# Quantile networks for two tiles at once, with the pieces ordered by a plan

## The chip, the cores and the metric

The kernel runs on one core of one Trainium2 chip. Times are device microseconds (us). The metric is the time of one execution, as the median of several runs; lower is better.

## The reference

The program has two layers on a graph of 4096 nodes with 128 features. Layer 0 is graph attention with 8 heads. Layer 1, where the change lies, takes for each node quantiles over a list of its neighbours, for each feature by itself:

```python
def _L1_gnn_ref(x, A, W, b):
    T, K = 5, 2
    QUANTILES, SELF_RATIO = (0.25, 0.5, 0.75), 0.5
    mask = A != 0
    rank = jnp.cumsum(mask.astype(jnp.int32), axis=1) - 1
    num_nbr = mask.sum(axis=1)
    skip = jnp.where(num_nbr > T, jnp.ceil(num_nbr / K).astype(jnp.int32), jnp.int32(1))
    remove = mask & ((rank + 1) % skip[:, None] == 0)
    keep = mask & ~remove
    n_keep = keep.sum(axis=1)
    vals = jnp.where(keep[:, :, None], x[None, :, :], big)
    svals = jnp.sort(vals, axis=1)
    for q in QUANTILES:
        idx = jnp.maximum(jnp.ceil(q * n_keep).astype(jnp.int32) - 1, 0)
        agg = agg + (1 / 3) * take_along_axis(svals, idx)
    agg = where(n_keep > 0, agg, 0)
    agg = (1.0 - SELF_RATIO) * agg + SELF_RATIO * x
    return agg @ W.T + b + x
```

The adjacency matrix holds a neighbour with probability 1/128, so a node has some 32 neighbours, and a kept list has some 22 to 62 entries.

## The kernel before

Two thirds of the program (searching the adjacency matrix for neighbours, building lists, attention, layer norm) are not touched by the change. They end with the rows of layer 0 written to `x1_d` in memory, and with index lists `idx`, where the nodes have been ordered by their number of neighbours and cut into 32 tiles of 128 nodes. Tile `t` has lists of `2 * HT[t]` places, from 22 (tile 0) over 24 to 42 (tile 30) to 62 (tile 31); shorter lists are padded.

The last stage takes one tile after another. POOL issues one indirect gather for each place of the list (`gather`, L186): each brings one row of 128 floats to each of the 128 partitions, one *slot* of the tile's buffer `vals`. `xs` is the nodes' own row. Five buffers of 42 slots, and one of 62 called `most`, are in rotation; a tile is gathered when an earlier one is done.

A selection network (`selection_network`) then brings the few places that can be a quantile (the *targets*, 3 to 5 for most tiles, 12 and 14 for the shortest and the longest lists) into order. It has 15 or 21 stages. A stage compares slot `i` with slot `i + d` for a set of `i`; where both results are needed later the minimum goes to `i` and the maximum to `i + d` (a two-ended piece, two instructions), else only one is computed. `groups` joins neighbouring slots to regular patterns and `pieces_of` cuts these into pieces of at most `TURN` = 12 slots. For each piece, ACT first copies the low slots to a buffer `low` in PSUM (L1162; left out for one-ended pieces of under 4 slots), and DVE compares `low` with the high slots in place (L1166). `low` comes from a pool of two buffers.

At a tile's end (L1175 to L1188) ACT multiplies each target slot by a weight (0 or a share of 1/6 for each node), and `xs` by 0.5; PE adds these products up by matmuls with the identity (`st_ps`), ACT copies the sum out (`sT`), PE multiplies by the layer's weights and adds `xs` and the bias (`fo_ps`), ACT copies the result (`o`), and POOL scatters it to the output (L195).

All engines run this stage in the order in which the program is written (`manual_schedule`). The order comes from generators: `quantile_out` yields after each stage of the network, and the loop takes turns between up to two running tiles. The second one begins when the first has at most 8 turns left. So where two tiles run, one stage of one is followed by one stage of the other, on ACT as on DVE, and between a tile's last stage and its products there is a stage of the other tile.

Of the kernel before, what the change touches and what calls it, by code (L numbers as in the profile page):

```python
# [9 lines left out]
F32 = mybir.dt.float32  # L10
# [3 lines left out]
ALU = mybir.AluOpType  # L14
AX = mybir.AxisListType
PSUM = bass.MemoryType.PSUM
# [8 lines left out]
P = 128  # L25
N = 4096
D = 128
H = 8
NT = N // P
# [31 lines left out]
    31, 32, 32, 33, 33, 34, 34, 35, 35, 36, 36, 37, 38, 39, 40, 42,  # L61
]
HT = [(c - 1) // 2 for c in CAP]
LMAX = 2 * max(HT)
LMOST = 2 * sorted(HT)[-2]
TURN = 12


R_NUM, R_OWN, R_F1 = L, L + 1, L + 2
# [18 lines left out]
def selection_network(n, targets):  # L88


    t = (n - 1).bit_length()
    stages = []
    p = 1 << (t - 1)
    while p:
        q, r, d = 1 << (t - 1), 0, p
        while True:
            stages.append((d, [i for i in range(n - d) if i & p == r]))
            if q == p:
                break
            d, q, r = q - p, q >> 1, p  # L100
        p >>= 1
    live = set(targets)
    plan = []
    for d, lows in reversed(stages):
        mins = [i for i in lows if i in live]
        maxs = [i for i in lows if i + d in live]
        used = set(mins) | set(maxs)
        touched = used | {i + d for i in used}
        plan.append((d, mins, maxs, sorted(live - touched)))
        live |= touched  # L110
    return plan[::-1]


def groups(slots):

    runs = []
    for s in slots:
        if runs and s == runs[-1][0] + runs[-1][1]:
            runs[-1][1] += 1
        else:  # L120
            runs.append([s, 1])
    out = []
    i = 0
    while i < len(runs):
        b, n = runs[i]
        j = i + 1
        stride = n
        if j < len(runs) and runs[j][1] == n:
            stride = runs[j][0] - b
            while j < len(runs) and runs[j] == [b + stride * (j - i), n]:  # L130
                j += 1
        out.append((b, j - i, stride, n))
        i = j
    return out


def pieces_of(g):


    b, k, stride, n = g  # L140
    if k == 1:
        parts = -(-n // TURN)
        out = []
        for i in range(parts):
            m = (n - sum(p[3] for p in out)) // (parts - i)
            out.append((b, 1, m, m))
            b += m
        return out
    if n >= TURN:
        return [p for i in range(k) for p in pieces_of((b + i * stride, 1, n, n))]  # L150
    parts = -(-k // (TURN // n))
    out = []
    for i in range(parts):
        kk = (k - sum(p[1] for p in out)) // (parts - i)
        out.append((b, kk, stride, n))
        b += kk * stride
    return out


def slots_of(tile_, g):  # L160

    b, k, stride, n = g
    if k == 1:
        return tile_[:, b : b + n, :].rearrange("p s d -> p (s d)")
    v = tile_[:, b : b + (k - 1) * stride + n, :]
    flat = v.rearrange("p s d -> p (s d)")

    return bass.AP(
        tensor=flat.tensor,
        offset=flat.offset,  # L170
        ap=[list(flat.ap[0]), [stride * D, k], [1, n * D]],
    )


def quantile_slots(t):


    ht = HT[t]
    slots = {ht - 1}
    for h in range((LOW[t] + 1) // 2 - 1, ht + 1):  # L180
        slots |= {ht - h + (h + 1) // 2 - 1, ht - h + (3 * h + 1) // 2 - 1}
    return slots


def gather(nc, dst, rows, idx):
    nc.gpsimd.indirect_dma_start(  # L186
        out=dst,
        out_offset=None,
        in_=rows,
        in_offset=bass.IndirectOffsetOnAxis(ap=idx, axis=0),  # L190
    )


def scatter(nc, rows, src, idx):
    return nc.gpsimd.indirect_dma_start(  # L195
        out=rows,
        out_offset=bass.IndirectOffsetOnAxis(ap=idx, axis=0),
        in_=src,
        in_offset=None,
    )  # L200
# [9 lines left out]
def kernel(  # L210
# [15 lines left out]
    nc = tc.nc  # L226
# [10 lines left out]
    ident = const.tile([P, P], F32, name="ident")  # L237
# [197 lines left out]
    kp.release()  # L435


    order = sorted(range(NT), key=lambda t: HT[t])
    order = order[0::2] + order[1::2][::-1]
    with tc.tile_pool(name="late", bufs=1) as late, tc.tile_pool(name="sort", bufs=5) as sp, tc.tile_pool(  # L440
        name="fin", bufs=3
    ) as fp, tc.tile_pool(name="low_ps", bufs=2, space=PSUM) as lp, tc.tile_pool(
        name="fin_ps", bufs=1, space=PSUM
    ) as pp, tc.manual_schedule(engines=ALL):
        wt = late.tile([P, NT, LMAX], F32, name="wt")
        slot_weights(tc, late, jp1, picks, wt)
        waiting = list(order)
        lists, running, outs = [], [], []

        def fetch_list():  # L450
            t = waiting.pop(0)
            n = 2 * HT[t]
            if n > LMOST:
                vals = sp.tile([P, LMAX, D], F32, name="most", bufs=1)
            else:
                vals = sp.tile([P, LMOST, D], F32, name="vals")
            for j in range(n):
                gather(nc, vals[:, j, :], x1_d, idx[:, t, j : j + 1])
            xs = fp.tile([P, D], F32, name="xs", bufs=6)
            gather(nc, xs, x1_d, own_i[:, t : t + 1])  # L460
            lists.append((t, vals, xs))

        def begin():
            t = lists[0][0]
            stages = len(selection_network(2 * HT[t], quantile_slots(t)))
            work = quantile_out(
                tc, lp, fp, pp, *lists.pop(0), wt, ident, ones, WlT, vecs[:, 3, :], outs
            )
            running.append([work, stages])

        for _ in range(5):
            fetch_list()
        while running or lists:
            if lists and (not running or (len(running) == 1 and running[0][1] <= 8)):
                begin()
            for one in list(running):
                one[1] -= 1
                if next(one[0], True):
                    running.remove(one)
                    while outs:  # L480
                        t, o = outs.pop(0)
                        scatter(nc, out, o, own_i[:, t : t + 1])
                    if waiting:
                        fetch_list()


    flag = nc.values_load(total[0:1, 0:1], min_val=0, max_val=1 << 20)  # L487
    with tc.If(flag > 0):
# [650 lines left out]
        )  # L1139


def quantile_out(tc, lp, fp, pp, t, vals, xs, wt, ident, ones, WlT, bl_b, outs):


    nc = tc.nc
    targets = sorted(quantile_slots(t))
    for d, mins, maxs, _ in selection_network(2 * HT[t], targets):
        lows, highs = set(mins), set(maxs)
        kinds = (
            (sorted(lows & highs), (0, d)),  # L1150
            (sorted(lows - highs), (0,)),
            (sorted(highs - lows), (d,)),
        )
        for slots, ends in kinds:
            for g in (p for whole in groups(slots) for p in pieces_of(whole)):
                b, k, stride, m = g
                low, high = slots_of(vals, g), slots_of(vals, (b + d, k, stride, m))
                if k * m >= 4 or len(ends) == 2:
                    kept = lp.tile([P, TURN * D], F32, name="low")[:, 0 : k * m * D]
                    if k > 1:  # L1160
                        kept = kept.rearrange("p (k d) -> p k d", k=k)
                    nc.scalar.copy(kept, low)  # L1162
                else:
                    kept = low
                for end in ends:
                    nc.vector.tensor_tensor(  # L1166
                        high if end else low, kept, high, ALU.max if end else ALU.min
                    )
        yield

    st_ps = pp.tile([P, P], F32, name="st_ps")
    terms = [(vals[:, j, :], wt[:, t, j : j + 1]) for j in targets] + [(xs, 0.5)]
    for i, (v, w) in enumerate(terms):
        u = fp.tile([P, D], F32, name="u", bufs=4)
        nc.scalar.mul(u, v, w)  # L1175
        nc.tensor.matmul(  # L1176
            st_ps, lhsT=u, rhs=ident, start=(i == 0), stop=(i == len(terms) - 1)
        )
    yield
    sT = fp.tile([P, P], F32, name="sT")  # L1180
    nc.scalar.copy(sT, st_ps)
    o_ps = pp.tile([P, D], F32, name="fo_ps")
    nc.tensor.matmul(o_ps, lhsT=sT, rhs=WlT, start=True, stop=False)
    nc.tensor.matmul(o_ps, lhsT=ident, rhs=xs, start=False, stop=False)
    nc.tensor.matmul(o_ps, lhsT=ones[0:1, :], rhs=bl_b[0:1, :], start=False, stop=True)
    yield
    o = fp.tile([P, D], F32, name="o")
    nc.scalar.copy(o, o_ps)  # L1188
    outs.append((t, o))


def general_attention(tc, x, adj, wa, x1_d, f2T_d, consts):
# [223 lines left out]
```

## Time and profile before

| what | us |
|---|---|
| median of 3 runs (3865.35 to 3875.0) | 3873.15 |
| the profiled execution | 3874.47 |
| its span, first to last instruction | 3872.7 |
| DVE busy in the span | 2613.9 |
| POOL busy | 2320.1 |
| ACT busy | 1204.0 |
| PE busy | 747.5 |

The span is cut into 40 slices of 96.8 us. The last stage's first gather is issued at 2047.2 us from the span's start, and its first compare starts at 2076.3. In the page and in the answers of the trace, a row names line, engine and operation, then what is written and read with the number of elements on each of 128 partitions; then the count, and busy time and mean duration. A wait names what ended it.

### The profile page before, as it was taken

To read this page: it belongs to the slowest core of one execution; us is meant where nothing else is said; L and a number is where in the kernel's file an instruction comes from. 1 tells how busy PE (TensorE), PEld (TensorE's weight loads), DVE (VectorE), ACT (ScalarE), POOL (GpSimd) and SP (SyncE) were. 2 spreads that over 40 slices of the span, in tenths; PEclk is the share of its full clock that TensorE was granted. 3 is DMA by queue.
4 is the path that set the end of the run, shared out by engine and by line. 5 is a ranking of instruction groups with operands and counts; after the bars stand their busy time and mean duration, and the time that the engine had idled before them with its cause. 6 is when DMAs were issued, how large, how long until landed. Compare 5 with 4: busy or idle time off the path is not lost. (4 is left out here: it accounts for less than half of the span.)

```text
span 3872.7 us, 17731 instructions
## 1 busy us (share of the span) xinstructions
PE 747.5 (19%) x2799; PEld 466.1 (12%) x2801; DVE 2613.9 (67%) x4953; ACT 1204.0 (31%) x1902; POOL 2320.1 (60%) x2452
## 2 busy tenths in 40 slices
PE   2023143334303231334330110000000010000001
PEld 1011022112202211111220100000000000000001
DVE  6798366657702111522214899999999999999987
ACT  3132123324102122221222433434444444344343
POOL 0676177777736677777756777777763345455520
PEclk9966566557656665666665555555555555555555
DMA  5542234334212122222211111111110011111100
GB/s 182 145 154 76 86 97 128 108 99 118 50 38 49 47 49 49 63 55 57 56 43 46 52 52 52 52 52 52 52 47 25 24 27 39 29 36 40 42 17 3
DMA packets 114202, 241.10 MB, mean 62 GB/s; under 512 B 50880, under 2 KB 67264, under 8 KB 105888
## 3 DMA queue, kind: packets, MB, share of 16 engines
q0 software_dynamic: 76224, 161.01, 16.5%
q10 hardware_dynamic: 12160, 68.49, 5.1%
q1 hardware_dynamic: 25696, 10.38, 1.3%
q14 instruction: 96, 0.79, 0.1%
q8 instruction: 26, 0.43, 0.0%
HBM read 228.53 MB, written 11.18 MB: 62 GB/s over the span
## 5 line engine op out<-in xcount | busy, mean ns | idle before, releaser
L1166 DVE TENSOR_TENSOR vals<-low,vals 128x1024 f32<-128x1024 f32 (+9 forms) x1359 | 1403.0, 1058 | 178.8 <-ACT low L1162 106.1
L186 POOL DMA_INDIRECT G<-xt_d,idx x1096 | 1099.1, 1003 | 470.0 <-issue 325.6
L186 POOL DMA_INDIRECT vals<-x_d,idx x960 | 911.6, 950 | 294.9 <-issue 283.4
L1162 ACT COPY low<-vals 128x1024 f32<-128x1024 f32 (+10 forms) x701 | 607.0, 876 | 983.5 <-DVE vals L1166 925.9
L888 PE MATMUL y<-G,pf 128*64 128x258 f32 (+1 forms) x1184 | 249.3, 492 | 837.6 <-DVE pf L866 765.1
L1176 PE MATMUL st_ps<-ident,u 128*128 128x128 f32 x344 | 83.3, 427 | 1662.5 <-ACT u L1175 1559.5
L195 POOL DMA_INDIRECT out_dram<-o,own_i x32 | 31.8, 993 | 467.2 <-ACT o L1188 462.0
L852 DVE TENSOR_TENSOR z<-G,f1x 128x256 f32<-128x256 f32 (+3 forms) x44 | 21.9, 498 | 418.7 <-DMA G<-xt_d,idx 411.2
L1176 PEld LDWEIGHTS st_ps<-ident,u 128*128 128x128 f32 x344 | 73.8, 320 | 1671.3 <-ACT u L1175 1567.9
L901 ACT COPY raw<-y 32x258 f32<-32x258 f32 (+1 forms) x472 | 172.2, 365 | 315.2 <-PE y L888 219.1
L854 ACT ACTIVATE z<-z 128x256 f32<-128x256 f32 (+3 forms) x60 | 20.0, 334 | 804.1 <-DVE z L853 804.1
L888 PEld LDWEIGHTS y<-G,pf 128*64 128x64 f32 (+1 forms) x1184 | 134.8, 183 | 940.9 <-DVE pf L866 753.1
L589 DVE MAX8 first<-sgn 128x8 f32<-128x128 bf16 x1024 | 209.5, 276 | 1.9
L561 ACT ACTIVATE sgn<-adj_t 128x2048 bf16<-128x2048 int32 x64 | 122.0, 1906 | 152.6 <-DVE first L589 118.0
L792 DVE TENSOR_SCALAR bad<-R 128x1 f32<-128x1 f32 x32 | 4.6, 145 | 209.9 <-DMA R<-rec_d 209.9
L1166 DVE TENSOR_TENSOR most<-low,most 128x1024 f32<-128x1024 f32 (+7 forms) x116 | 131.9, 1167 | 2.6 <-ACT low L1162 0.7
L195 POOL DMA_INDIRECT rec_d<-rec,ranks x32 | 30.9, 967 | 156.1 <-DVE ranks L732 100.1
L949 PE MATMUL o<-hv,W_sb 128*128 128x256 f32 (+1 forms) x208 | 85.9, 537 | 196.2 <-DVE hv L943 196.2
L1166 DVE TENSOR_TENSOR vals<-vals 128x256 f32<-128x256 f32 (+2 forms) x335 | 119.0, 410 | 0.0
L908 DVE TENSOR_SCALAR rden<-raw 128x8 f32<-128x8 f32 x32 | 6.7, 208 | 163.2 <-ACT raw L901 163.2
L601 DVE MAX8 rec<-first 128x8 f32<-128x256 f32 x256 | 108.7, 425 | 6.6
L921 ACT COPY yT<-turned 128x512 f32<-128x512 f32 x64 | 65.3, 1020 | 153.6 <-PE turned L920 147.7
(180 smaller groups left out, 1841.2 us busy)
## 6 DMA issues: line engine op xcount, KB each, us to landing
adj_t<-in_adj_dram ACTq DMA_DIRECT2D x64, 1024.0 KB
G<-xt_d,idx POOLq DMA_INDIRECT x1096
vals<-x_d,idx POOLq DMA_INDIRECT x960
R<-rec_d SPq DMA_DIRECT2D x128, 26.4 KB
xt_d<-rec SPq DMA_DIRECT2D x4, 548.0 KB
rec<-in_x_dram SPq DMA_DIRECT2D x4, 512.0 KB
score<-rec_d SPq DMA_DIRECT2D x120, 1.0 KB
Gs<-xt_d,idx POOLq DMA_INDIRECT x88
```

Source lines behind the costliest of these rows:

```text
L186: nc.gpsimd.indirect_dma_start(out=dst, out_offset=None, in_=rows, in_offset=bass.IndirectOffsetOnAxis(ap=idx, axis=0),)
L195: return nc.gpsimd.indirect_dma_start(out=rows, out_offset=bass.IndirectOffsetOnAxis(ap=idx, axis=0), in_=src, in_offset=None,)
L561: nc.scalar.activation(sgn, adj_t, AF.Sign, accum_out=cnt[:, i : i + 1])
L589: nc.vector.max(first[:, ts(c0 // CW + c, 8)], key[:, b * (512 // CW) + c, :])
L601: nc.vector.max(top, first)
L888: nc.tensor.matmul(yv[p0 : p0 + m], lhsT=pf[:, c : c + m], rhs=rhs, start=(i == 0), stop=(i == len(parts) - 1), skip_group_check=True,)
L901: nc.scalar.copy(raw[p0 : p0 + m, 4 * half + b - 1 : 4 * half + b + 1, :], y[p0 : p0 + m, :, a : a + D + 1],)
L921: nc.scalar.copy(yT[:, :, ts(place, P)].rearrange("p h (u g) -> p g u h", u=4)[:, ts(half, 16)], t_ps.rearrange("p b (g u h) -> p (b g) u ...
L949: nc.tensor.matmul(o, lhsT=consts["W1_sb"][:, h, :], rhs=hv[:, ts(j, n)], start=(h == 0), stop=(h == H - 1),)
L1162: nc.scalar.copy(kept, low)
L1166: nc.vector.tensor_tensor(high if end else low, kept, high, ALU.max if end else ALU.min)
L1176: nc.tensor.matmul(st_ps, lhsT=u, rhs=ident, start=(i == 0), stop=(i == len(terms) - 1))
```

## The change

The 32 tiles are put into 19 units: tiles 0, 1, 30, 31, 2 and 3 each by itself, the others two by two. Both tiles of a unit get lists of one length (the longer), lie in one buffer behind one another, and use one network, with the targets of both. A piece holds the same slots of both tiles, up to `TURN` = 14 slots in all, in one instruction; a pattern that would need more pieces that way is cut for each tile by itself. The condition for a copy (at least 4 slots, or two-ended) counts the slots of both tiles.

When the program is built, `plan_units` lays down the order of everything with a small model: what a copy, a compare and a gather take, when each slot is ready, and a ring of two copy buffers. Of the pieces of the current stages of at most two running units it takes the one for which DVE would wait least, the older unit first. When a unit is done, its sums are placed at once, the second half (`turn`) six pieces later, the output copy (`emit`) twelve pieces later, and the next unit's gathers are placed. Output scatters stand among later gathers, one for every fourth. Three buffers of 80 slots take the place of the six. The two copy buffers are halves of one PSUM tile `low`, used by turns; sums and results of both tiles of a unit share one PSUM tile `fin`. `EARLY` is empty, so that `first_stage` is never called.

```diff
+UNITS = [(0,), (1,), (30,), (31,)] + [(t, t + 1) for t in range(28, 3, -2)] + [(2,), (3,)]
+for u in UNITS:
+    for t in u:
+        HT[t] = max(HT[v] for v in u)
 LMAX = 2 * max(HT)
-LMOST = 2 * sorted(HT)[-2]
-TURN = 12
+ROOM = max(2 * HT[u[0]] * len(u) for u in UNITS)
+TURN = 14
+EARLY = []
...
+def stages_of(tiles):
+    n = 2 * HT[tiles[0]]
+    targets = sorted(set().union(*(quantile_slots(t) for t in tiles)))
+    stages = []
+    for d, mins, maxs, _ in selection_network(n, targets):
...
+            for g in groups(slots):
+                whole = [(tuple(range(len(tiles))), p) for p in pieces_of(g, TURN // len(tiles))]
+                apart = [((i,), p) for i in range(len(tiles)) for p in pieces_of(g, TURN)]
+                for who, p in whole if len(whole) <= len(apart) else apart:
+                    stage.append((who, p, d, ends))
+        stages.append(stage)
+    return n, targets, stages
+
+COPY, COMPARE, FETCH, LAND = (150, 107), (110, 133), 1250, 2200
...
+    def best():
+        found = None
+        for r, u in enumerate(running):
+            for p, (who, g, d, ends) in enumerate(todo[u][0]):
+                spots = slots_in(who, g)
+                low = max(at[u, i, s] for i, s in spots)
+                ready = max(at[u, i, s + d] for i, s in spots)
+                copied = len(spots) >= 4 or len(ends) == 2
+                if copied:
+                    done = max(clock["act"], low + 100, ring[0]) + COPY[0] + COPY[1] * len(spots)
+                    ready = max(ready, done + 100)
+                else:
+                    done = clock["act"]
+                    ready = max(ready, low)
+                key = (max(ready - clock["dve"], 0), r, p)
+                if found is None or key < found[0]:
+                    found = (key, u, copied, done)
+        return found
...
+        (late, _, p), u, copied, done = best()
+        who, g, d, ends = todo[u][0].pop(p)
+        events.append(("piece", u, who, g, d, ends, copied))
...
+        if not todo[u]:
+            running.remove(u)
+            events.append(("sums", u))
+            tails += [[count + 6, "turn", u], [count + 12, "emit", u]]
+            clock["act"] = max(clock["act"], clock["dve"]) + 300 * len(UNITS[u]) * (len(plans[u][1]) + 1)
+            free[home[u]] = clock["act"] + 1000
+            if loaded < len(UNITS):
+                load()
...
-    order = sorted(range(NT), key=lambda t: HT[t])
-    order = order[0::2] + order[1::2][::-1]
-    with tc.tile_pool(name="late", bufs=1) as late, tc.tile_pool(name="sort", bufs=5) as sp, tc.tile_pool(
-        name="fin", bufs=3
-    ) as fp, tc.tile_pool(name="low_ps", bufs=2, space=PSUM) as lp, tc.tile_pool(
+    with tc.tile_pool(name="late", bufs=1) as late, tc.tile_pool(name="sort", bufs=3) as sp, tc.tile_pool(
+        name="fin", bufs=2
+    ) as fp, tc.tile_pool(name="low_ps", bufs=1, space=PSUM) as lp, tc.tile_pool(
...
+        plans, events = plan_units(3)
+        work, outs, turn = {}, [], 0
+        low = lp.tile([P, 2, TURN * D], F32, name="low")
+        for kind, u, *rest in events:
+            tiles = UNITS[u]
+            n, targets, stages = plans[u]
+            if kind == "load":
+                vals = sp.tile([P, ROOM * D], F32, name="vals")
...
+                        gather(nc, dst, x1_d, idx[:, t, j : j + 1])
...
+                        if outs and count % 4 == 0:
+                            scatter(nc, out, *outs.pop(0))
+                    gather(nc, xs[:, i, :], x1_d, own_i[:, t : t + 1])
...
+            elif kind == "piece":
+                compare(nc, low[:, turn % 2, :], work[u][0], n, *rest)
+                turn += rest[-1]
+            elif kind == "sums":
+                vals, _, xs, _ = work[u]
+                fin = pp.tile([P, 4, P], F32, name="fin")
+                for i, t in enumerate(tiles):
+                    terms = [
+                        (slots_of(vals, n, (i,), (j, 1, 1, 1)), wt[:, t, j : j + 1]) for j in targets
+                    ] + [(xs[:, i, :], 0.5)]
+                    for a, (v, w) in enumerate(terms):
+                        g = fp.tile([P, D], F32, name="u", bufs=12)
+                        nc.scalar.mul(g, v, w)
+                        nc.tensor.matmul(fin[:, i, :], lhsT=g, rhs=ident, ...)
...
+def compare(nc, room, vals, n, who, g, d, ends, copied):
+    b, k, stride, m = g
+    low, high = slots_of(vals, n, who, g), slots_of(vals, n, who, (b + d, k, stride, m))
+    kept = low
+    if copied:
+        kept = room[:, 0 : len(who) * k * m * D]
...
+        nc.scalar.copy(kept, low)
+    for end in ends:
+        nc.vector.tensor_tensor(high if end else low, kept, high, ALU.max if end else ALU.min)
```

## The prediction

> **What bounds the kernel now.** First the page: whole-span shares, then the slices.
>
> ```profile
> PE 747.5 (19%) x2799; PEld 466.1 (12%) x2801; DVE 2613.9 (67%) x4953; ACT 1204.0 (31%) x1902; POOL 2320.1 (60%) x2452
> ...
> DVE  6798366657702111522214899999999999999987
> ```
>
> DVE works 67% of the span, but from slice 23 on (2227 us) its digit is 9: the last stage, the quantile networks, is DVE's. So I read that stage by stretches (columns PE, PEld, DVE, ACT, POOL).
>
> ```profile
> 2076.00:2400.00 324.00, 27.83 (x108) 23.00 (x108) 282.09 (x312) 125.34 (x174) 245.59 (x258) 0.51 0.20 52
> 2400.00:3780.00 1380.00, 100.58 (x380) 83.06 (x380) 1284.65 (x1415) 572.33 (x767) 762.11 (x802) 0.51 0.14 38
> 3780.00:3862.00 82.00, 8.30 (x33) 6.98 (x33) 73.05 (x98) 30.49 (x50) 1.91 (x2) 0.54 0.00 2
> ```
>
> From the first compare (2076) to the last (3861) DVE works 1639.8 of 1786 us; ACT and POOL have a third to spare. DVE sets the end: 11 us after its last compare the span is over. The waits of the stage (sum, times, longest):
>
> ```profile
> ACT low L1162 <- DVE vals L1166: 954.1, 532, 19.8
> ...
> DVE vals L1166 <- ACT low L1162: 106.1, 135, 4.5
> ...
> DVE vals L1166 <- DMA vals<-x_d,idx: 45.8, 2, 36.0
> ```
>
> ACT waiting for DVE is harmless. DVE waiting for ACT's copies, 106.8 us with the long tile's 0.7, is what an order can win; of the 45.8 behind gathers, 36.0 precede the first compare and stay.
>
> **What one piece costs.** The groups by shape:
>
> ```profile
> L186 POOL DMA_INDIRECT vals<-x_d,idx x919 | 872.9, 950 | 280.6 <-issue 271.2 <-DMA vals<-x_d,idx 6.4 <-DVE vals L1166 3.1
> L1166 DVE TENSOR_TENSOR vals<-low,vals 128x1024 f32<-128x1024 f32 x536 | 646.0, 1221 | 53.1 <-ACT low L1162 32.8 <-DMA vals<-x_d,idx 9.8
> L1162 ACT COPY low<-vals 128x1024 f32<-128x1024 f32 x266 | 267.9, 1015 | 339.7 <-DVE vals L1166 324.4 <-DMA vals<-x_d,idx 8.0 <-DVE most L1166 7.0
> ...
> L1166 DVE TENSOR_TENSOR vals<-vals 128x256 f32<-128x256 f32 x188 | 70.4, 418 | 0.0
> ```
>
> A slot is 128 elements: from 2 to 8 slots a compare grows by (1221-419)/6 = 133.7 ns a slot. Walking the network code for all 32 tiles gives 1823 compares of 10,766 slots and 761 copies, just the counts in the trace. Of the 1786 us, 106.8 + 9.8 are waits and 1439 is slots (10,766 x 0.1337); the other 230 us are 126 ns for each instruction. The same walk over the changed lists, in 19 units: 1383 compares of 10,881 slots, 714 copies of 5692 (before 5149).
>
> **1. Fewer, larger compares.** 440 compares fewer x 0.126 = -55; 115 slots more (equal list lengths) x 0.134 = +15: -40. 168 of those removed are one-ended pieces, cheaper than the mean (two `vals<-vals` of 256 lie 0.33 apart, only 0.07 above their slots), so I take **-37** (-54 to -30). [...]
>
> **2. Sums of two tiles right behind a unit's last compare.** ACT is in order. A tile's end now:
>
> ```profile
> 2678.87 0.75 DVE L1166 TENSOR_TENSOR vals<-vals 128x128 f32<-128x128 f32 x2
> 2679.54 1.41 DVE L1166 TENSOR_TENSOR vals<-low,vals 128x512 f32<-128x512 f32 x2
> ...
> 2679.72 1.28 ACT L1175 ACTIVATE u<-vals,wt 128x128 f32<-128x128 f32 x4 [2.53 <-DVE vals L1166]
> ...
> 2681.00 0.31 ACT L1175 ACTIVATE u<-xs 128x128 f32<-128x128 f32 x1
> 2681.22 1.43 ACT L1162 COPY low<-vals 128x1536 f32<-128x1536 f32 x1
> ...
> 2682.68 1.76 DVE L1166 TENSOR_TENSOR vals<-low,vals 128x1536 f32<-128x1536 f32 x1 [1.74 <-ACT low L1162]
> ```
>
> The tile's last compare ends at 2679.62. ACT then multiplies (four plus one, 0.32 us apart), then copies the other tile's next piece; DVE is covered by one pair (1.41) and idles 1.74. I sum all gaps over 0.1 us at the 31 such ends: 40 us, 4.5 of it at the longest list with its 15 products. In the new order (I walked what follows what, and took no time from the planner's clock) the sums stand directly after the last compare: no copy for the other unit is ahead of them, so the cover is gone, and a double unit has 8 to 12 products. With 2 early, 8 x 0.32 + 0.1, then a copy of 4 to 12 slots (0.59 to 1.44): 3.7 x 13 = 48. The single units: 13 and 15 products 5.8 and 6.0, the others 2.9, 3.2 and 2.3: 20. Together 68, **+27** (10 to 40).
>
> **3. The order.** DVE's other gaps sum to 84: 29 up to 2400, 55 later. At the start units 0, 1 and 30 run nearly alone (30's first piece needs its last gather, at 2161, when 0 and 1 are done): some 7 each as for the first tile now, 26 with 31 and a gather. Later two units hide each other's copies; 2 us per unit for its last small stages is 26, and 5 for the tail. One loss: pairs of 2-slot one-ended pieces, which needed no copy, become 4-slot ones that do; ACT at 0.66 a copy against DVE's 0.60 costs some 0.07 each, 89 times, 6. So 63 instead of 84: **-21** (0 to -50).
>
> **4. Two copy buffers in one PSUM tile.** `low` is [2, 14*128] floats: a half is 7168 bytes, 3.5 banks of 2 KB, so the halves share the fourth bank. Now each buffer is 12 slots, three whole banks. The second half always touches the shared bank, the first half with 14 slots only; by the walked order that is 20 of the 40 14-slot pieces. Are accesses kept apart by byte or by bank? A nearby row:
>
> ```profile
> 1456.50 1.12 PE L981 MATMUL turned<-ident,hv 128*128 128x128 f32 x4
> ...
> 1457.66 0.29 DVE L987 TENSOR_TENSOR x<-turned,R 128x128 f32<-128x128 f32 x1 [1.99 <-PE turned L981]
> ```
>
> Four transposes write four quarters of one bank; DVE reads the first quarter, done after about a quarter of 1.12 us, only once all four are over (1457.62). [...] the trace has only PE against DVE. By byte this costs 0. By bank each of the 20 is bared twice: its own copy (1.65, the 12-slot row plus two slots) waits for the compare before it, and the next copy (0.59 to 1.65) for its own compare: with 0.1 each, 20 x 1.76 + 27 = 62, less what step 3 counts already: **+57** (0 to 65). I take the bank. Were the whole tile one region, all 714 copies would lie bare: 1.0 each, some +700.
>
> **5. Covered parts.** POOL: 1028 + 32 gathers and 32 output scatters x 1.25 (0.95 and its 0.30 gap) = 1365 us beside some 1830 of DVE. A load starts when a unit frees one of three buffers: 31 to 102 us, against the next unit's 32 to 141 of compares; the short singles lie at the ends, where loads are ahead. If that cover failed, a late load would cost up to 20. The scatters move among later gathers, behind `o` copies long done; the last three units' come at the end as now. ACT: 5692 x 0.107 + 714 x 0.16 = 723 (672 now), free two thirds of the time. PE gets 7 products more. The ending (products, two matmul groups, scatter) keeps its 11 us.
>
> **Sum**: -37 + 27 - 21 + 57 = +26, against the profiled execution (span 3872.7, 3874.5 with its launch, 1.3 above the median); on the median, 3899.
>
> **The rivals.**
> *The buffers are independent, guarded by byte.* Then step 4 is 0: -31, **3842**, faster. It is decided at 20 places; up to about 7 bared pairs the change gains by more than can be told. For it: the plan works with two free buffers. Against: the row at 1457.66.
> *The order does nothing*: the gaps stay at 84, or three buffers make loads late by some 20 at the start: +47, **3920**. For it: two tiles already interleave now, with 1.4 us of gaps in 2900 to 3100.
> *The order does more*: half of the ends' and later gaps go: -31 further, **3868**, no change. Against: no copy stands ahead of the sums.
> *One region*: **4570**. Against: the second half would never have served.
>
> **How the numbers follow.** About 0.3% (11.6 us) is what a measurement here can tell from no change. The sum as worked out has 0.55: slower 0.42, same 0.11, faster 0.02. By byte 0.19: faster 0.15, same 0.04. The order does more, 0.08: 0.04 faster, 0.03 same, 0.01 slower. It does nothing, 0.15: slower 0.14, same 0.01. One region, 0.03, slower. Together faster 0.21, same 0.19, slower 0.60. The likeliest case alone reaches from 3875 to 3925 (its steps' bounds, not all at one end); 3832 to 3945 takes in most of the byte case and of the idle order, and leaves the tails and the one region out.
>
> **What would show it.** 1383 compares and 714 copies; DVE's busy time in the stage lower by some 37 to 40. Waits of DVE for `low` near 190 us, with 40 gaps of 0.7 to 1.8 around 14-slot compares (step 4; without them, by byte), and 3 to 6 us at each unit's end (step 2). DVE still at 9 in the slices, and no long wait for gathers after 2200. Wrong would be: waits for `low` below 107, waits for gathers over 20, or busy DVE time that has not fallen.

## The result, and the profile after

The changed kernel takes 4558.6 us (median of 4 runs, 4554.98 to 4563.11) against 3874.07 (median of 4, 3865.35 to 3879.51): a ratio of 1.177, with a 95% interval of 1.1746 to 1.1795. The forecast was 3899, in a range of 3832 to 3945. The sign was right and the size was wrong by 660 us; what happened is the rival "one region", put at 4570 and given 0.03.

The page of the profile, which is of an execution of 4559.52 us (span 4557.7), shows it in two lines:

```profile
PE 744.4 (16%) x2813; PEld 465.9 (10%) x2815; DVE 2633.4 (58%) x4513; ACT 1257.6 (28%) x1836; POOL 2320.4 (51%) x2458
...
DVE  6894757663212241215666666666666666666666
```

DVE's busy time has risen by 19.5 us in the whole span (2613.9 before), which explains nothing of 684. But the digits of the last stage, which were 9, are 6: in that stage DVE stands idle a third of the time. The stretches say the same (columns PE, PEld, DVE, ACT, POOL):

```profile
2076.00:2400.00 324.00, 17.51 (x66) 14.82 (x66) 222.11 (x221) 97.91 (x127) 245.09 (x260) 0.51 0.19 52
2400.00:4400.00 2000.00, 106.40 (x420) 90.57 (x420) 1335.00 (x1062) 635.43 (x732) 757.07 (x801) 0.51 0.10 26
4400.00:4558.00 158.00, 17.36 (x64) 14.46 (x64) 101.61 (x100) 49.45 (x72) 8.25 (x9) 0.51 0.01 5
```

In the middle 2000 us DVE works 1335 and ACT 635, together 1970: the two take turns. The waits from 2030 on (sum, times, longest) name the partners:

```profile
ACT low L1334 <- DVE vals L1336: 1661.1, 690, 4.1
...
DVE vals L1336 <- ACT low L1334: 780.7, 685, 4.5
...
DVE vals L1336 <- DMA vals<-x_d,idx: 44.8, 7, 36.0
```

DVE waits for ACT's copies 685 times, and ACT waits for DVE before 690 of its 714 copies. The third row is what it was: gathers are not the matter. The timeline shows one turn after another (start, duration, then in brackets the idle time of the engine just before):

```profile
2606.78 1.02 ACT L1334 COPY low<-vals 128x1024 f32<-128x1024 f32 x1 [2.55 <-DVE vals L1336]
2607.83 2.48 DVE L1336 TENSOR_TENSOR vals<-low,vals 128x1024 f32<-128x1024 f32 x2 [1.08 <-ACT low L1334]
2610.35 1.44 ACT L1334 COPY low<-vals 128x1536 f32<-128x1536 f32 x1 [2.55 <-DVE vals L1336]
2611.82 3.55 DVE L1336 TENSOR_TENSOR vals<-low,vals 128x1536 f32<-128x1536 f32 x2 [1.51 <-ACT low L1334]
2615.41 1.44 ACT L1334 COPY low<-vals 128x1536 f32<-128x1536 f32 x1 [3.62 <-DVE vals L1336]
```

Each copy starts 0.04 us after the compare of the piece before has ended, and each compare 0.03 us after its own copy. With two buffers the copy at 2610.35 should have run beside the compare at 2607.83. Over the whole stage only 47 of the 714 copies overlap a compare in time; in the kernel before 708 of 761 do.

Of the stage from the first compare to the last (2074.3 to 4546.7, so 2472.4 us; 1785.2 before) I made three sums: the compares' durations less their overlap and with the gaps under 0.1 us ("the stream"), the gaps over 0.1 us at the ends of units or tiles, and those elsewhere.

| us | before | after | difference |
|---|---|---|---|
| the stream of compares | 1665.4 | 1680.4 | +15 |
| waits for copies at ends | 33.6 | 64.2 | +31 |
| other waits for copies | 73.9 | 717.4 | +644 |
| gaps for other reasons | 12.4 | 10.4 | -2 |

The stream, which should have become 37 shorter, is 15 longer. That is the same cause: before, compares standing back to back overlapped by 75.7 us in all, and where every piece waits only 8.0 of that is left.

### The profile page after: what moved, and what is told of

Same layout as the page of the kernel before. It is cut to its first block, busy times and chain, and to the rows that moved or that the text cites. A ratio compares the mean times of both kernels' runs of the same rounds, so it can differ in the third digit from the quotient of the medians.

```text
span 4557.7 us, 16892 instructions
## 1 busy us (share of the span) xinstructions
PE 744.4 (16%) x2813; PEld 465.9 (10%) x2815; DVE 2633.4 (58%) x4513; ACT 1257.6 (28%) x1836; POOL 2320.4 (51%) x2458
## 5 line engine op out<-in xcount | busy, mean ns | idle before, releaser
L1336 DVE TENSOR_TENSOR vals<-low,vals 128x1024 f32<-128x1024 f32 (+9 forms) x1292 | 1629.5, 1261 | 847.8 <-ACT low L1334 780.7
L322 POOL DMA_INDIRECT vals<-x_d,idx x1028 | 971.6, 945 | 1314.2 <-ACT u L623 912.4
L1334 ACT COPY low<-vals 128x1024 f32<-128x1024 f32 (+8 forms) x714 | 722.9, 1012 | 1713.8 <-DVE vals L1336 1661.1
L624 PE MATMUL fin<-ident,u 128*128 128x128 f32 x358 | 80.0, 413 | 2054.1 <-ACT u L623 2054.1
L624 PEld LDWEIGHTS fin<-ident,u 128*128 128x128 f32 x358 | 74.3, 316 | 2060.7 <-ACT u L623 1973.0
L1133 PE MATMUL key<-yT,W_sb 128*128 128x256 f32 (+1 forms) x208 | 98.0, 617 | 14.4 <-ACT yT L1094 14.4
L322 POOL DMA_INDIRECT Gs<-xt_d,idx x88 | 86.2, 980 | 26.8 <-issue 25.9
```

The source lines that it names most:

```text
L322: nc.gpsimd.indirect_dma_start(out=dst, out_offset=None, in_=rows, in_offset=bass.IndirectOffsetOnAxis(ap=idx, axis=0),)
L624: nc.tensor.matmul(fin[:, i, :], lhsT=g, rhs=ident, start=(a == 0), stop=(a == len(terms) - 1), skip_group_check=True,)
L1133: nc.tensor.matmul(hT[:, ts(j, n)], lhsT=consts["W_sb"][:, h, :], rhs=yT[:, h, 0:n], start=True, stop=True,)
L1336: nc.vector.tensor_tensor(high if end else low, kept, high, ALU.max if end else ALU.min)
```

## The experiments

On the chips of these runs the kernel before takes 4283 to 4331 us and not 3874: its last stage begins some 290 us later, and DVE stands still in it for about 160 us for which the profile names no partner. Durations of single instructions are the same (the 8-slot compare takes 1.22 us on both). No row tells why, so every run is read by its ratio to the kernel before on the same chip, and expectations given in us against 3874 are read as ratios to it. This is what DVE's waits look like there, in the unchanged kernel (`e9_before_here`):

```profile
DVE vals L1166 <- issue: 116.0, 49, 24.5
DVE vals L1166 <- ACT low L1162: 101.8, 83, 9.1
DVE vals L1166 <- DMA vals<-x_d,idx: 45.8, 2, 36.1
DVE vals L1166 <- remote: 30.6, 9, 6.3
DVE vals L1166 <- DVE vals L1166: 14.1, 19, 1.4
```

"issue", "remote" and the last row are the stand-stills, 160.7 in all. Most of them begin on ACT: of the 116.0 of "issue", 112.8 end as the compare's own copy ends, and the copy was late because ACT had stood still, as here:

```profile
2472.71 0.27 ACT L1181 COPY sT<-st_ps 128x128 f32<-128x128 f32 x1 [21.18 <-remote]
2472.88 1.24 ACT L1162 COPY low<-vals 128x1280 f32<-128x1280 f32 x1
...
2474.14 3.02 DVE L1166 TENSOR_TENSOR vals<-low,vals 128x1280 f32<-128x1280 f32 x2 [20.09 <-issue]
```

What ACT stands still for stays open. The second row of the table, 101.8, is the one that the change is about.

**Is it the one tile?** Four kernels were run on one chip. `e1_two_tiles` keeps everything of the change but takes `low` from a pool of two tiles, and cuts pieces to 12 slots so that each tile is three whole banks of PSUM, the memory in which `low` lies. The built programs show the banks: they place each PSUM tile at a numbered bank. The two tiles here, of 6144 bytes on each partition, are at banks 0 and 3, and the tile behind them, `fin`, at 6. In the changed kernel `low`, 14,336 bytes, is at bank 0 and `fin` at 7; so a bank there is 14,336 / 7 = 2048 bytes, and a half of `low` three and a half banks.

```diff
-TURN = 14
+TURN = 12
-    ) as fp, tc.tile_pool(name="low_ps", bufs=1, space=PSUM) as lp, ...
+    ) as fp, tc.tile_pool(name="low_ps", bufs=2, space=PSUM) as lp, ...
-        low = lp.tile([P, 2, TURN * D], F32, name="low")
...
-                compare(nc, low[:, turn % 2, :], work[u][0], n, *rest)
-                turn += rest[-1]
+                low = lp.tile([P, TURN * D], F32, name="low") if rest[-1] else None
+                compare(nc, low, work[u][0], n, *rest)
```

> The changed kernel with one thing undone: the two copy buffers are two PSUM tiles of 12 slots again, taken by turns from a pool of two (TURN = 12, which gives 1433 compares and 739 copies in place of 1383 and 714). Theory A (the halves of one PSUM tile are kept apart as one region, so each copy waits for the compare before it): DVE's waits for the copies fall from 781 us to some 100 to 130, and the time to 3830 to 3870, my sum of the prediction without its step 4. Theory B (only where the halves share a bank): the same here. Theory C (the new access patterns over both tiles of a unit in vals make the next copy wait for the compare): still some 680 waits, 4560 to 4600.

Measured: 4208.88, ratio 0.9698 [0.9648, 0.9748]. The change, with nothing altered but the buffers and the cut, is faster than the kernel before by 3%, where the expectation comes to 0.1 to 1.1%. The waits of DVE in the last stage:

```profile
DVE vals L1335 <- issue: 80.1, 35, 29.8
DVE vals L1335 <- ACT low L1333: 59.0, 29, 6.3
DVE vals L1335 <- DMA vals<-x_d,idx: 43.3, 3, 36.0
DVE vals L1335 <- remote: 37.5, 11, 6.6
DVE vals L1335 <- DVE vals L1335: 12.8, 17, 1.5
```

59.0 us for copies, where the changed kernel has 780.7; 53.6 of it at the units' ends. Of its 739 copies 697 overlap a compare.

`e2_one_tile_whole_banks` differs from the changed kernel in one number only, `TURN = 12`: one tile with two halves, each of three whole banks (`low` at bank 0, `fin` at 6), so that no bank is shared.

```diff
-TURN = 14
+TURN = 12
```

> The changed kernel with TURN = 12, low still one PSUM tile of two halves; a half is now 6144 bytes, three whole banks, so the halves share none. Theory A: no different from the changed kernel, 739 copies all bare, 4570 to 4610. Theory B: the waits go, 3830 to 3870 as with two tiles. Theory C: 4560 to 4600.

Measured: 4902.19, ratio 1.1304 [1.1244, 1.1364]. The halves lie on bank boundaries and the turns stay, by the timeline (the gap before a compare, 1.08 and 1.29, is its copy's time, whatever its releaser is called):

```profile
3303.49 1.02 ACT L1334 COPY low<-vals 128x1024 f32<-128x1024 f32 x1 [2.55 <-DVE vals L1336]
...
3304.54 2.48 DVE L1336 TENSOR_TENSOR vals<-low,vals 128x1024 f32<-128x1024 f32 x2 [1.08 <-issue]
...
3307.05 1.23 ACT L1334 COPY low<-vals 128x1280 f32<-128x1280 f32 x1 [2.55 <-DVE vals L1336]
...
3308.31 3.02 DVE L1336 TENSOR_TENSOR vals<-low,vals 128x1280 f32<-128x1280 f32 x2 [1.29 <-ACT low L1334]
```

Of the 739 copies 46 overlap a compare. So it is not the shared bank, on which the prediction stood. Between this run and `e1_two_tiles`, neither the order of pieces, nor their sizes, nor the number of banks differs: only whether the program declares one tile or two. What that does can be read in the built programs, where each instruction carries the semaphore counts that it waits for. With one tile, 720 of the 739 copies wait for the count that the latest compare from `low` before them raises (695 of 714 in the changed kernel). With two tiles 125 do, and 579 wait only for an earlier count; the few others carry no such wait themselves.

`e3_before_one_tile` does the reverse: the kernel before, with its two buffers made halves of one tile, each three whole banks (`low` at bank 0, `st_ps` at 6).

```diff
-    ) as fp, tc.tile_pool(name="low_ps", bufs=2, space=PSUM) as lp, ...
+    ) as fp, tc.tile_pool(name="low_ps", bufs=1, space=PSUM) as lp, ...
+        both = [lp.tile([P, 2, TURN * D], F32, name="low"), 0]
...
-                    kept = lp.tile([P, TURN * D], F32, name="low")[:, 0 : k * m * D]
+                    kept = lp[0][:, lp[1] % 2, 0 : k * m * D]
+                    lp[1] += 1
```

> The kernel before with one part of the change alone: low is one PSUM tile of two halves (12 slots, three whole banks each), used by turns; nothing else. Theory A: its 761 copies (672 us busy, some 0.05 us of passing on each) lie bare, +550 to +650 us over 3874, that is 4420 to 4520. Theory B and theory C: 3874, no change.

Measured: 4840.93, ratio 1.1173 [1.112, 1.1226]. The one edit makes the kernel before 510 us slower, and only 108 of its 761 copies overlap a compare. DVE's waits for copies go to 522.3 us, and another 146.5, in 147 waits, stand under "issue" but end as the compare's own copy ends: bare copies too. The 510 is less than the 550 to 650 expected. A likely reason, which was not tested, is the chip's own stand-stills: the kernel before has some 160 us of them to lose here, and time that DVE stands still anyway now falls within a wait for a copy.

`e4_tiles_14_and_12` keeps pieces of 14 slots, in two tiles, one of 14 and one of 12 slots (at banks 0 and 4, `fin` at 7), with pieces over 12 slots always in the larger.

```diff
-        low = lp.tile([P, 2, TURN * D], F32, name="low")
+        sides = [lp.tile([P, m * D], F32, name=f"low{m}") for m in (TURN, TURN - 2)]
...
+                slots = len(rest[0]) * rest[1][1] * rest[1][3]
+                if rest[-1] and slots > TURN - 2:
+                    turn = 0
+                compare(nc, sides[turn % 2], work[u][0], n, *rest)
                 turn += rest[-1]
```

> The changed kernel with TURN = 14 kept and the two copy buffers as two PSUM tiles, one of 14 slots (four banks) and one of 12 (three banks); a piece of more than 12 slots always takes the large one. Theory A: as with two tiles of 12, less 50 compares (6 us), plus some 10 to 20 us where a 14-slot piece takes the large tile twice running: 3830 to 3880. Theory B: the same. Theory C: 4540 to 4580.

Measured: 4276.21, ratio 0.9861 [0.9815, 0.9907]. It is faster than before by 1.4%, but slower than `e1_two_tiles`: a 14-slot piece may have to take the buffer that was used last, and DVE's waits for copies are 88.5 us; one stand-still of 34 us is in it too.

**Does only PSUM have it?** The changed kernel with its one `low` tile of two halves in SBUF, the memory in which `vals` lies.

```diff
-        low = lp.tile([P, 2, TURN * D], F32, name="low")
+        low = late.tile([P, 2, TURN * D], F32, name="low")
```

> The changed kernel (TURN = 14) with low as one tile of two halves in SBUF in place of PSUM, nothing else. Theory A1 (only a PSUM tile is kept apart as a whole; an SBUF tile by what is touched, as vals is): DVE's waits for the copies fall to 60 to 110 us and the time to that of two PSUM tiles, within 40 us (a compare reads both sides from SBUF then, as the vals<-vals rows do, which are no slower). Theory A2 (any tile of which halves are used is one region): as the changed kernel, over 4850.

Measured: 4229.43, ratio 0.9779 [0.9731, 0.9828]. DVE waits 54.9 us for copies, and 679 of the 714 copies overlap a compare. One tile used by halves is therefore kept apart by halves in SBUF and not in PSUM (47 of 714 in the changed kernel). The kernel is not the fastest, though: DVE waits 183.8 us for gathers, 36.0 of it ahead of the first compare; the last section comes to that.

**Both kernels on one chip.** With the same chip's before in `e9_before_here`:

> The kernel before, unchanged, for its profile on these chips, where it takes 4330 us and not 3874. If the difference is the engines' standing still with no cause in the profile, its first compare starts some 300 us later than the 2076 of the first profile, and the last stage is some 150 longer with DVE waiting 100 to 150 us for nothing shown; its waits for the copies stay at 100 to 110 us and its compares keep their durations.

Measured: 4314.24, ratio 0.9996 [0.9979, 1.0013], no difference, as it must be.

> The changed kernel, unchanged, on the same chip. Theory A: its 714 bare copies cost the same here, +650 to +720 us against e1_two_tiles, 4860 to 4930, ratio to the kernel before 1.12 to 1.14.

Measured: 4874.26, ratio 1.1281 [1.123, 1.1331]. The loss is 558 us here and 684 on the first chip. DVE's gaps of the last stage for copies and stand-stills are 802.0 in this run (576.3 for copies, and 225.7 "issue", 173 of whose 174 waits end as the compare's own copy ends, so that they are bare copies too) and 262.5 in the kernel before beside it (the four `vals` rows above but gathers); on the first chip 780.7 and 106.1. The gaps of the changed kernel are nearly the same on both; it is the kernel before that has the stand-stills to lose.

**What the rest of the change is worth.** With two tiles, I undid one part at a time, beside `e1_two_tiles` once more:

> The kernel of e1_two_tiles once more (low as two PSUM tiles of 12 slots, all else as changed), because the engines of that chip stood still for stretches in which the profile shows no cause. Theory A (the one PSUM tile was the whole loss): 0 to 40 us below the kernel before, as my sum without its step 4 has it (31, less 6 for 50 compares more at TURN = 12). If those stretches made the gain of 122 us there, it is not found again; if it is real, it stands at about 120 here too.

Measured: 4217.26, ratio 0.9748 [0.9711, 0.9785]. It is 109 us below the kernel before; 122 had been measured in `e1_two_tiles`, and 0 to 40 were expected. The larger gain is found again.

The sums of a unit were then placed two pieces later, with what follows them:

```diff
-            events.append(("sums", u))
-            tails += [[count + 6, "turn", u], [count + 12, "emit", u]]
...
+            tails += [[count + 2, "sums", u], [count + 8, "turn", u], [count + 14, "emit", u]]
...
```

> As e5_two_tiles_again, with a unit's sums (and with them its output and the next load) placed two pieces later in the order, so that two copies of the other unit stand ahead of the products on ACT. Theory D (step 2: the sums right behind the last compare bare the products and the next copy, some 64 to 71 us over all unit ends): DVE's gaps at the ends fall below 20 us and the time by 40 to 55 us against e5. Rival (DVE catches up elsewhere, or the later loads starve it): less than 15 us.

Measured: 4192.92, ratio 0.9685 [0.9653, 0.9717]: 24 us less than the version beside it, half of what I had expected. The ends did what was meant. Here is one, with the products of two tiles, first DVE in the timeline, then ACT:

```profile
3307.00 90.95 DVE L1336 TENSOR_TENSOR vals<-low,vals 128x768 f32<-128x768 f32 x73
```

```profile
3306.78 1.02 ACT L1334 COPY low<-vals 128x1024 f32<-128x1024 f32 x1 [0.29 <-DVE vals L1336]
3307.98 1.02 ACT L1334 COPY low<-vals 128x1024 f32<-128x1024 f32 x1 [0.18 <-DVE vals L1336]
3308.93 1.27 ACT L623 ACTIVATE u<-vals,wt 128x128 f32<-128x128 f32 x4
3310.11 0.29 ACT L623 ACTIVATE u<-xs 128x128 f32<-128x128 f32 x1
3310.31 1.26 ACT L623 ACTIVATE u<-vals,wt 128x128 f32<-128x128 f32 x4
3311.48 0.29 ACT L623 ACTIVATE u<-xs 128x128 f32<-128x128 f32 x1
3311.68 2.10 ACT L1334 COPY low<-vals 128x1024 f32<-128x1024 f32 x2
```

The copies at 3306.78 and 3307.98 stand ahead of the products, DVE has compares to go on with, and its run of 73 instructions from 3307.00 has no gap. Over all ends the waits for copies fell from 53.6 to 4.2. But elsewhere they rose from 7.0 to 40.3, of which 16.8 and 14.8 are two stalls behind an output copy `o` for which ACT itself had to wait 18.8 and 17.0 us. The profile gives "remote" as what released it; I have not settled what.

Next the model's choice by waiting time was taken away; of the pieces in reach, always the first of the older unit is taken:

```diff
-                key = (max(ready - clock["dve"], 0), r, p)
+                key = (r, p)
```

> As e5_two_tiles_again, with the planner's choice by lateness taken out: always the older unit, its pieces in the order of its stages; the second unit never fills in. Theory E (step 3: it is the filling in from a second unit that hides the copies at the starts of stages): 19 units x 15 to 21 stages x 0.5 to 1.0 us, +150 to +300 us against e5. Rival (the pieces within one stage hide each other's copies well enough): below +60.

Measured: 4251.33, ratio 0.9835 [0.9805, 0.9864]: 34 us slower than the version beside it and still 1.7% faster than before. Expected were 150 to 300, so that theory fell: with two free buffers the pieces of one stage hide each other's copies here, and the other waits for copies are 44.2 us and not hundreds.

Last, all units single:

```diff
-UNITS = [(0,), (1,), (30,), (31,)] + [(t, t + 1) for t in range(28, 3, -2)] + [(2,), (3,)]
+UNITS = [(0,), (1,), (30,), (31,)] + [(t,) for t in range(29, 1, -1)]
...
-    with ... tc.tile_pool(name="sort", bufs=3) as sp, ...
+    with ... tc.tile_pool(name="sort", bufs=4) as sp, ...
```

> As e5_two_tiles_again, with each tile a unit by itself (1823 compares, 761 copies, lists of their own length; four buffers, two fin tiles): the planned order without the networks for two tiles. Theory of step 1 (126 ns for each compare saved, 134 for each slot more): 390 compares more are +49, 115 slots less are -15, and 32 ends in place of 19, each with 5 products, cost some 15 more: +40 to +65 us against e5, so about the kernel before. Rival (the gain is the order's alone): +-15 of e5.

Measured: 4221.38, ratio 0.978 [0.9742, 0.9817], within 4 us of the version with pairs. By the sums of its trace pairs are worth more: without them the stream is 1660.9 and not 1631.9, the ends 70.3 and not 53.6, the other waits 14.0 and not 7.0, together 53 us. But its stand-stills sum to 84 and not 124 ("issue", "remote" and DVE itself), on the same chip, and why is not known. The time is what the rival expected, that the gain is the order's alone; whether the pairs add to it, this run does not decide.

**The best of both.** Four buffers in SBUF, pieces of 14 slots, and the sums two later:

```diff
-    ring = [0, 0]
+    ring = [0, 0, 0, 0]
...
-            ring = [ring[1], clock["dve"] + 50]
+            ring = ring[1:] + [clock["dve"] + 50]
...
+                low = sp.tile([P, TURN * D], F32, name="low", bufs=4) if rest[-1] else None
```

> As e6_sums_two_later, with TURN = 14 and low as four tiles of 14 slots in SBUF, used by turns, and the plan's ring of copy buffers four long: ACT may run up to four pieces ahead. Theory A (buffers that are free let the plan work) and theory D (copies ahead of the sums cover the products): DVE's waits for the copies, 44 us in e6, fall below 20, 50 compares fewer save 6: 10 to 40 us below e6, ratio to the kernel before 0.955 to 0.968. Rival (what is left is standing still, which moves elsewhere, or compares from SBUF are slower): 0.968 to 0.98.

Measured: 4165.25, ratio 0.9731 [0.9709, 0.9752] (before on that chip: 4283.08). It is not better than the 0.9685 of `e6_sums_two_later`, and short of what I expected. Copies are hardly waited for any more, gathers are:

```profile
DVE vals L1336 <- DMA vals<-x_d,idx: 215.0, 17, 36.0
...
DVE vals L1336 <- ACT low L1334: 9.3, 13, 2.1
```

Of the 215.0, 36.0 lie ahead of the first compare, as in every version; 179.0 are new. They do not all come on top: the stand-stills, 124.5 us in `e6_sums_two_later`, are 6.0 here. All gaps between the first and the last compare sum to 195 us here and 171 there.

So the version to keep is, by its ratio, `e6_sums_two_later`: two PSUM tiles of 12 slots and the sums two pieces later. (Against the last version that is a comparison over two chips, with intervals that touch.) It beats the kernel before by 3.15% and the changed one by more than 14% (0.9685 / 1.1281 = 0.859, over two chips).

## Why the prediction was wrong

**Step 4 failed, by some 700 us.** It asked whether accesses to the two halves are kept apart by byte or by bank, took the bank, and charged 20 pieces, +57. In the trace all pairs are bared: the other waits for copies stand at 717.4, where they are 6 to 7 with free buffers, and the stream has +15 instead of the -32 that it gives with free buffers, since the overlap is lost. That is 711 and 47, some 758 in place of 57. The forecast's sign rested on this step alone: without it the sum was -31, and with two tiles the change is in fact faster. "Slower" came out right by a wait that was thirteen times what had been charged for it. The row that I rested it on, four matmuls to one bank and a read that starts at 1457.66, after all four (1457.62), can't tell bank from tile: the four quarters are also one tile, `turned`, of 2048 bytes, which the built program places at bank 6. And the row has PE and DVE; that ACT and DVE are held apart by banks was not shown. "One region" was written down and worked out well (4570; its 714 bare copies at 1.0), but I put it aside because "the second half would never have served". That says what the author of a plan wanted, not what the program does. No row of the trace of before excluded it, and it was worth ten times the next uncertainty.

What the runs show of the cause: the same bytes in the same number of banks are serialized as one tile (46 of 739 copies overlap a compare in `e2_one_tile_whole_banks`) and not as two (697 of 739 in `e1_two_tiles`), and one tile by halves in SBUF is not serialized (679 of 714). The wait therefore comes from how the program is told which accesses depend on which, by tiles in PSUM. It is a wait that the program carries: with one tile the copies carry one for the latest compare (720 of 739), and with two most of them do not (125 of 739). Whether the chip's memory would hold up accesses to one tile or one bank by itself is not shown; no run here used one tile with waits placed by hand. Whether two tiles that share a bank would cost the +57 was not tried.

**Step 1 held.** 1383 compares and 714 copies were counted in the trace. With free buffers and `TURN = 12` there are 50 compares more, 6 us by the 126 ns each, so -31 was to be had; the stream of `e1_two_tiles` is 1632.2 against 1664.4 in `e9_before_here`: -32. The 126 ns, worked out from the stage of the kernel before, was right for an instruction back to back. The -54 that bounded the step was the author's estimate; no run shows it. The 126 is itself a mean of two kinds. In the trace of before, the second compare of each of the 714 two-ended pieces waits for a semaphore of DVE itself and starts 34 ns after the first has ended; some 930 others start 83 ns before the one ahead of them has ended.

**Step 2 held** in the changed kernel. It has 64.2 us at the ends, forecast 68 (53.6 with two tiles); the difference to before is +31 by the table's count and was put at +27.

**Step 3 had the right sign and was three times too small**, as far as it can be seen where buffers are free. The forecast let the waits away from ends shrink by 21. They went from 78.0 (`e9_before_here`; 73.9 on the first chip) to 5.9 and 7.0 in `e1_two_tiles` and `e5_two_tiles_again`: -71. I had charged 7 us for each unit that runs alone at the start, and 2 us for the last stages of each unit; `e7_one_unit_at_a_time` shows why that was too much: even one unit by itself hides most of its copies (44.2 us of waits away from the ends). The rival "the order does more" was the better one here.

**Step 5 held.** Waits for gathers are 44.8 (45.8 before), 36.0 of it ahead of the first compare, and 43.3 in `e1_two_tiles`, where the compares leave less time to cover them.

Without step 4's failure the sum is -32 for the stream, +20 for the ends (53.6 against 33.6) and -71 for the other waits: -83, so some 3791 on the first chip. That is an estimate; the two-tile version was not run there. In ratio, 0.979, it promises less than the 0.970 and 0.975 that were measured; part of the difference is that the stand-stills came out shorter there too: 130.4 us in `e1_two_tiles` and 160.7 in `e9_before_here` (rows above).

## What to carry to other kernels

Give each buffer of a rotation in PSUM a tile of its own (ratio 0.970 with two tiles of 12 slots, 1.130 with one), and when a trace is there, look at one pair of neighbouring pieces: does the copy of the second run beside the compare of the first? A rotation that does not rotate shows as two engines whose busy times add up to the span (here 1335 and 635 us of 2000). When a mechanism is in doubt, price all granularities that it could have, and let the size of the worst one decide how much of the chance it gets; and put an in-order engine's extra work one or two pieces behind, where the engine it feeds still has work queued (two pieces gave 24 us here).

## What was not expected of the hardware

With both sides of a compare in SBUF, the gathers that POOL issues get slower, by a mean of 1291 against 961 ns. Here are the gathers of the last stage (count, then busy time and mean ns), in `e12_four_buffers_sums_later` and in `e6_sums_two_later`, which copies to PSUM:

```profile
L323 POOL DMA_INDIRECT vals<-x_d,idx x1028 | 1327.5, 1291 | 357.0 <-issue 307.9 <-ACT low L1334 37.5 <-ACT u L623 5.5
```

```profile
L323 POOL DMA_INDIRECT vals<-x_d,idx x1028 | 987.5, 961 | 681.4 <-ACT u L623 317.6 <-issue 308.7 <-ACT low L1334 48.4
```

The instructions are the same, and 330 ns have been added to the mean. It is not an even slowing. Of the gathers from 2380 to 3900 in the former 385 of 892 take under 1.05 us, as nearly all do in the latter (845 of 909), and 189 take over 1.5, against 7. A pair of neighbours shows it:

```profile
3000.41 12.17 DVE L1336 TENSOR_TENSOR vals<-low,vals 128x512 f32<-128x512 f32 x11 [16.28 <-DMA vals<-x_d,idx]
...
3002.95 0.95 POOL L323 DMA_INDIRECT vals<-x_d,idx  x1 [0.30 <-issue]
3004.20 1.97 POOL L323 DMA_INDIRECT vals<-x_d,idx  x1 [0.31 <-issue]
```

One of 0.95 us and one of 1.97. DVE was in its run of compares at that time, the 8-slot ones of which take 1.22 us in either kernel (1.219 and 1.223 in the groups by shape): POOL waits and DVE doesn't. `e11_one_tile_in_sbuf` has a mean of 1297 ns.

What POOL waits for can be read from where the slow gathers end. Of the 600 gathers over 1.0 us in `e12_four_buffers_sums_later`, 583 end 0.82 us (to within 0.012) after the end of a compare that was running when they began. The 144 gathers that meet no compare in their first 0.9 us take at most 0.98. The kernel before has the same in small, at the one-ended pieces without a copy, which also read both sides from SBUF: 31 of its 1022 gathers take over 1.0 us, all 31 end 0.82 us after such a compare, and the 921 that meet none take at most 0.97. One of the 31 follows. Of the three compares from 2608.16, the last begins at 2608.70 and ends at 2609.25; the gather ends at 2610.07:

```profile
2608.16 1.08 DVE L1166 TENSOR_TENSOR vals<-vals 128x256 f32<-128x256 f32 x3
2608.74 1.33 POOL L186 DMA_INDIRECT vals<-x_d,idx  x1 [0.30 <-issue]
```

So the slow gathers end by the clock of a compare with both sides in SBUF, 0.82 us after it, while the compare keeps its 1.22 us; how the chip brings this about is not shown. The copy into PSUM has a second use, then, which the prediction did not see though the trace of before has it: it leaves DVE with one SBUF input, and the gathers' mean is 961 ns and not 1291. With the buffers in SBUF DVE hardly waits for copies any more (9.3 us), but gathers are late: that is where the 179.0 us of new waits for them in `e12_four_buffers_sums_later` come from.
